# The first cross attention of a decoder: values and sums of a head in one product instead of two

## The chip, the cores and the metric

The kernel runs on one core of a Trainium2 chip. The metric is the device time of one launch in microseconds (us). Five runs of the kernel before took 1561.32 to 1566.45 us, with a median of 1562.86 us.

The engines are named as the profile names them: PE is the tensor engine (PEld its weight loads), DVE the vector engine, ACT the scalar engine, POOL the GpSimd engine, SP the engine that only issues transfers. SBUF is the working memory and PSUM the memory that the tensor engine writes; both have 128 partitions (rows).

## The reference, cut to what matters

The program is a two-layer decoder over 16 batches of 128 tokens and 256 features, in fp32. Layer 0 has a ternary self attention, a cross attention with rotary positions over the context and a mixture of experts; layer 1 has a latent attention, a second cross attention without projections and a gated product-key network. The change is in the cross attention of layer 0. There the input of a batch is read as 128 channels by 256 positions:

```python
q = jnp.einsum('oi,bit->bot', wq, x) + bq[None, :, None]
k = jnp.einsum('oi,bit->bot', wk, c) + bk[None, :, None]
v = jnp.einsum('oi,bit->bot', wv, c) + bv[None, :, None]
...
scores = jnp.einsum('bhqc,bhkc->bhqk', q, k) / math.sqrt(K_CHANNELS)
p_attn = jax.nn.softmax(scores, axis=-1)
out = jnp.einsum('bhqk,bhkc->bhqc', p_attn, v)
out = out.transpose(0, 1, 3, 2).reshape(b, CHANNELS, t_t)
out = jnp.einsum('oi,bit->bot', wo, out) + bo[None, :, None]
```

There are 16 heads of 8 channels, 256 queries and 256 keys. Query and key are turned by the rotary positions before the scores. The result is added to the input and normalised.

## The kernel before, in words

**Layout.** The 128 channels lie on the 128 partitions: four groups `g` of 32 rows, and in each group four heads of 8 rows. A score tile `ps_st` holds the transposed or plain scores of two groups and two heads. The transposed scores, with the row maximum already subtracted by a small product (`pick` and `nmT`), go through `Exp` on ACT (line 421) into `pT`, keys on partitions. The plain scores go only through a maximum on DVE (line 416), which fills `nm` for the next batch's subtraction.

**Sums.** For each unit `u` of a batch (a key half `kc`, a pair `i` of heads, one head `n` of the pair), `sums` (line 424) issues eight products into one PSUM tile `o` (`ps_o`), whose two halves are `o[:, 0, :]` for the weighted values and `o[:, 1, :]` for the sums of the weights. The first four (line 433), one for each group, have 32 columns of the value tile as stationary operand, in which only the 8 columns of this head are not zero; so the four heads of a group are gathered in the 32 rows of the group. The next four (line 437) have a tile of ones, `ones8`, in the place of the values, so that the sum of a head's weights stands on all 8 rows of that head. An fp32 product shows as two MATMUL records, so a unit shows as eight of `ps_o<-pT,v` and eight of `ps_o<-pT,ones`. A batch has eight units.

**Division.** `divided` (line 296) takes the logarithm of `o[:, 1, :]` on ACT (line 299), the exponential of its negative (line 300), and multiplies `o[:, 0, :]` by that on DVE (line 302) into `oT`, each over 256 elements a row. `cross_finish` (line 807) then multiplies by the output weights `xw[:, 5, :]`, and adds bias and input (line 811, `xn`); `normalised` (line 186) makes the new `x` with two statistics on DVE, a power on POOL (line 184) and a last DVE instruction (line 194).

**Values.** `values` (line 834) makes the projected values with PE and writes them with one DVE instruction (line 839) into one of three value tiles `v8`, whose other columns were zeroed by POOL at the start (line 75).

**The order of the work.** `by_beats` (line 242) writes the order out by hand. A batch of this attention takes eight beats, one for each unit. In a beat PE first makes scores for two batches (line 385): the transposed ones of one batch and the plain ones of a later one, by turns. Then come the sums of the unit whose scores were made two beats before, then the jobs of that beat. PE runs strictly in this order (`mm` and `turned`, lines 206 and 210). Of the jobs of line 853 each beat has one or two, and they return every eight beats. Here the beats of a batch period are lettered from the one with the division:

| beat | jobs | lines |
|---|---|---|
| A | last sums of a batch, then `divide`; `keys` of a later batch | 847, 831 |
| B | first sums of the next batch; `values` | 834 |
| C | `finish`, then the normalisation | 850 |
| D | `gate_turn`: turns the new `x` for the expert gate | 748 |
| E | `gate`: expert logits and the two best experts | 756 |
| F | `places`: where each token goes in the experts' lists | 782 |
| G | `maxima`: the maxima of a batch, split in three and turned | 844 |
| H | `queries` of a later batch | 824 |

DVE, ACT and POOL instructions are put in order by a planner at build time; on the chip each engine then works strictly in that order.

**What is shared.** The PSUM has eight banks. Score tiles rotate over three buffers of two banks each (line 235), two tiles a beat: a plain tile uses the buffer that the transposed tile of the beat before has left, so it waits for that tile's `Exp`; a transposed tile uses that of the plain tile two beats before and waits for its maximum. The jobs share one bank `ps_m`. The tile `o` has one buffer (line 227): the first sums of the next batch, in beat B, wait until the division has read `o` for the last time.

Of the kernel before, what the change touches and what calls it, by code (L numbers as in the profile page):

```python
# [18 lines left out]
P = 128  # L19
# [10 lines left out]
def kernel(ctx: ExitStack, tc: tile.TileContext, a: dict, out: bass.AP):  # L30
# [36 lines left out]
    def head_columns(pool, keys, heads, name, count=4):  # L67


        hd = 32 * 4 * (2 if keys == 1 else 1) // heads  # L70
        per = 32 // hd
        tiles = []
        for n in range(count):
            t = pool.tile([P, heads // per * keys, per * (32 + hd)], F32, name=f"{name}_{n}")
            nc.gpsimd.memset(t, 0.0)
            tiles.append(t)
        return tiles

    def max_columns(pool, name):

        tiles = []
        for n in range(2):
            t = pool.tile([P, 2, P], BF16, name=f"{name}_{n}")
            nc.gpsimd.memset(t, 0.0)
            tiles.append(t)
        return tiles
# [15 lines left out]
    causT = const.tile([P, P], BF16, name="causT")  # L102

    ones16 = const.tile([P, 2, 32], F32, name="ones16")
    ones8 = const.tile([P, 4, 32], F32, name="ones8")
    for t, per in ((ones16, 2), (ones8, 4)):
        nc.gpsimd.memset(t, 0.0)
        for i in range(per):
            nc.gpsimd.memset(t[:, i, i * 32 // per : (i + 1) * 32 // per], 1.0)

    v16 = head_columns(cpool, 1, 16, "v16")
    nmx = max_columns(cpool, "nmx")
# [10 lines left out]
    )  # L123
    onesb = const.tile([P, P], BF16, name="onesb")
    nc.gpsimd.memset(onesb, 1.0)
    v8 = head_columns(w0, 2, 16, "v8", 3)
    iota8 = const.tile([P, 8], F32, name="iota8")
    nc.gpsimd.iota(iota8, [[1, 8]], base=0, channel_multiplier=0, allow_small_or_imprecise_dtypes=True)

# [9 lines left out]
    nc.gpsimd.memset(zero, 0.0)  # L139


    xw = load(cpool, [P, 6, P], a["xw"], "xw", eng=nc.gpsimd)
    xb = load(cpool, [P, 5], a["xb"], "xb", eng=nc.gpsimd)
    bv2 = load(cpool, [P, D], a["bv2"].partition_broadcast(P), "bv2", eng=nc.gpsimd)
    rope = load(cpool, [P, 2, D], a["rope"], "rope", eng=nc.gpsimd)
# [60 lines left out]
    def mm(*args, **kw):  # L206

        tc.keep_in_program_order(nc.tensor.matmul(*args, **kw))  # L208
# [64 lines left out]
    def own_columns(t, hd):  # L273

        return t.rearrange("p g (i w) -> p g i w", w=32 + hd)[:, :, :, 0:hd]
# [20 lines left out]
    def divided(pl, o):  # L296
# [5 lines left out]
        nc.vector.tensor_tensor(oT.rearrange("p c q -> p (c q)"), o[:, 0, :], r, ALU.mult)  # L302
        return oT

    def rows_of(g):
        return slice(32 * g, 32 * g + 32)

# [71 lines left out]
    def cross_scores(pl, heads, kept):  # L379


        per = heads // 4
        onez = ones8 if per == 4 else ones16

        def beat(s, t):
            if t:
# [37 lines left out]
        def sums(b, u):  # L424
            z = kept[b]
            if u == 0:
                z["o"] = pl["o"].tile([P, 2, D], F32, name="ps_o")
            o, n = z["o"], u % 2
            kc, i = divmod(u // 2, per // 2)
            pTs = [z["pT"][u - n], z["pT"][u - n + 1]]  # L430
            first, last = u == 0, u == heads // 2 - 1
            for g in range(4):
                mm(
                    o[rows_of(g), 0, :], lhsT=z["v"][:, 4 * kc + g, 32 * (2 * i + n) : 32 * (2 * i + n) + 32],
                    rhs=pTs[g // 2][:, g % 2, n, :], start=first, stop=False,
                )
            for g in range(4):
                mm(
                    o[rows_of(g), 1, :], lhsT=onez[:, 2 * i + n, :], rhs=pTs[g // 2][:, g % 2, n, :],
                    start=False, stop=last,  # L440
                )

# [361 lines left out]
                in_offset=None,  # L804
            )

    def cross_finish(pl, b, oT):
        po = pl["m"].tile([P, D], F32, name="ps_m")
        mm(po, lhsT=xw[:, 5, :], rhs=oT.rearrange("p c q -> p (c q)"), start=True, stop=True)
        xn = pl["w"].tile([P, D], F32, name="xn")  # L810
        nc.vector.scalar_tensor_tensor(xn, po, xb[:, 4:5], x_t[b], ALU.add, ALU.add)
        normalised(x_t[b], xn)

    def rope_cross_plain(pl):
# [42 lines left out]
    def rope_cross_masked(st):  # L857
# [3 lines left out]
        for b in range(B):  # L861
# [19 lines left out]
            cross_finish(pl, b, oT)  # L881
            for part in (gate_turn, gate, places):
                part(pl, b)

# [533 lines left out]
def layouts(inputs):  # L1418
# [15 lines left out]
    masks += [((row % 32 < 12) & (row % 4 == j)) * 1.0 for j in range(4)]  # L1434
    wq, wk, wv, wo = (i[f"L0_xattn_w{n}"] for n in "qkvo")
    bq, bk, bo = (i[f"L0_xattn_b{n}"] for n in "qko")
    mask = i["mask_1x1x2048x2048_if1"][0, 0]
    return {
        "x": i["x"],
# [7 lines left out]
        "xw": np.stack([wq.T, wq[mate].T, wk.T, wk[mate].T, wv.T, wo.T], 1),  # L1447
# [45 lines left out]
```

## Time and profile before

| what | value |
|---|---|
| median of five runs | 1562.86 us |
| the profiled execution | 1564.26 us |
| its span, first to last instruction | 1562.1 us |
| PE busy | 1408.4 us (90%) |
| DVE busy | 807.9 us (52%) |
| ACT busy | 555.3 us (36%) |
| POOL busy | 265.6 us (17%) |
| first cross attention, scores to last placement | about 170 to 590 us |
| one batch period in it, beat A to beat A | 23.42 us |

The span is what lies between the first and the last instruction; 2.2 us of the profiled execution lie around it. The busy shares are means over the whole program, in which the attentions (to about 590 us, and from 960 to 1300 us), the experts (600 to 900 us) and the last network follow each other. A MATMUL's recorded end is modelled, and neighbouring products overlap, so the steps of PE are read from start to start.

### The profile page before, as it was taken

The numbers are of one execution on the slowest core, as the hardware profiler recorded it, in microseconds if no ns is written. First come the engines' busy times: TensorE is split into PE (matmuls) and PEld (weight loads), VectorE is DVE, ScalarE is ACT, GpSimd is POOL, SyncE is SP. The second block draws the span as 40 slices with busy tenths as digits, with TensorE's granted clock in tenths as the row PEclk, the third lists the DMA queues.
The fourth block names the chain that finished last, engine by engine and source line by source line (L and its number), as shares of the span: only waits on it lengthen the run. The fifth ranks groups of instructions, "written<-read, shape, count | busy, mean of one in ns | idle before, by whom it ended". The sixth has DMA issues, their size and how long they took to land. (4 is left out here: it accounts for less than half of the span.)

```text
span 1562.1 us, 30539 instructions
## 1 busy us (share of the span) xinstructions
PE 1408.4 (90%) x13003; PEld 880.4 (56%) x13003; DVE 807.9 (52%) x2210; ACT 555.3 (36%) x939; POOL 265.6 (17%) x370
## 2 busy tenths in 40 slices
PE   4999889999999977999999859899899998989997
PEld 3666545555555534777777636555555544446756
DVE  6788767677677630011111046776666655553322
ACT  1444334444444431111111124443355554772010
POOL 7001122332332210000000043321111200000000
PEclk9999989999999997999999959999999998999999
DMA  8200000000000005233320141100000000000000
GB/s 290 74 2 2 2 1 8 15 15 9 15 15 8 15 15 180 88 94 111 95 92 34 36 139 29 28 9 2 1 2 2 2 2 1 1 0 8 21 4 24
DMA packets 41689, 58.16 MB, mean 37 GB/s; under 512 B 4752, under 2 KB 31392, under 8 KB 41408
## 3 DMA queue, kind: packets, MB, share of 16 engines
q1 hardware_dynamic: 35984, 41.95, 8.2%
q0 software_dynamic: 4720, 13.29, 2.6%
q8 instruction: 106, 1.74, 0.5%
q10 hardware_dynamic: 832, 0.79, 0.2%
q14 instruction: 47, 0.39, 0.1%
HBM read 39.24 MB, written 16.78 MB: 36 GB/s over the span
## 5 line engine op out<-in xcount | busy, mean ns | idle before, releaser
L416 DVE TENSOR_REDUCE nm<-ps_st 128x4 f32<-128x1024 f32 x192 | 233.9, 1222 | 98.0 <-PE ps_st L208 97.5
L421 ACT ACTIVATE pT<-ps_st 128x1024 f32<-128x1024 f32 x192 | 196.5, 1023 | 246.5 <-PE ps_st L208 246.5
L184 POOL TENSOR_TENSOR rstd<-ve,nhalf 128x1 f32<-128x1 f32 x112 | 62.5, 558 | 713.3 <-DVE ve L183 697.2
L208 PE MATMUL ps_o<-pT,v 128*32 128x256 f32 (+1 forms) x2560 | 165.2, 347 | 1.1 <-DVE oT L302 0.8
L208 PE MATMUL ps_o<-pT,ones 128*32 128x256 f32 x2048 | 158.5, 380 | 0.0
L943 DVE TENSOR_TENSOR ye<-ps_e,b 128x256 f32<-128x256 f32 x40 | 17.0, 425 | 265.1 <-PE ps_e L940 265.1
L208 PE MATMUL ps_st<-rot,z 32*128 32x256 f32 x1024 | 147.5, 408 | 5.1 <-DVE nm L416 4.7
L928 PE MATMUL ps_h<-h,w 128*128 128x320 f32 x512 | 139.1, 432 | 0.0
L932 ACT ACTIVATE h<-ps_h,b 128x640 f32<-128x640 f32 x64 | 50.7, 793 | 228.7 <-PE ps_h L928 228.7
L208 PE MATMUL ps_st<-z,rot 32*128 32x512 f32 x512 | 131.9, 592 | 0.0
L928 PEld LDWEIGHTS ps_h<-h,w 128*128 128x128 f32 x512 | 97.3, 190 | 40.5
L208 PE MATMUL ps_st<-nmT,pick 32*128 32x256 bf16 x1024 | 103.7, 275 | 18.0 <-ACT nmT L293 15.7
L208 PEld LDWEIGHTS ps_o<-pT,v 128*32 128x32 f32 x2560 | 55.2, 109 | 104.4 <-issue 87.4
L208 PEld LDWEIGHTS ps_st<-rot,z 32*128 32x128 f32 x1024 | 89.5, 188 | 11.8 <-DVE nm L416 5.5
L352 DVE TENSOR_REDUCE nm<-ps_st 128x8 f32<-128x1024 f32 x64 | 78.1, 1220 | 34.5 <-PE ps_st L208 34.5
L1039 POOL DMA_INDIRECT y<-ys,place x32 | 31.1, 973 | 313.0 <-DVE absT L1031 305.3
L208 PEld LDWEIGHTS ps_o<-pT,ones 128*32 128x32 f32 x2048 | 65.7, 110 | 33.0
L208 PEld LDWEIGHTS <-pick 32*128 32x128 bf16 x1024 | 33.5, 91 | 83.0 <-issue 76.3
L928 PE MATMUL ps_h<-xeT,w 128*128 128x320 f32 x256 | 72.9, 443 | 2.3 <-DVE xeT L918 1.1
L208 PE MATMUL ps_st<-ctx,z 32*128 32x256 f32 x512 | 72.1, 398 | 0.5 <-DVE nm L416 0.4
L940 PE MATMUL ps_e<-w,h 128*128 128x256 f32 x320 | 70.4, 379 | 0.0
L208 PE MATMUL ps_f<-fxT,fgw 128*128 128x512 f32 x128 | 62.7, 613 | 6.7 <-ACT g L1215 6.7
(271 smaller groups left out, 2437.3 us busy)
## 6 DMA issues: line engine op xcount, KB each, us to landing
w<-in_W_dram SPq DMA_DIRECT2D x16, 512.0 KB, 4.1
w<-in_W_dram SPq DMA_DIRECT2D x8, 1024.0 KB, 5.3
xs<-zero SPq DMA_DIRECT2D x40, 128.0 KB, 4.7
xe<-xs SPq DMA_DIRECT2D x40, 128.0 KB, 3.7
ys<-ye SPq DMA_DIRECT2D x40, 128.0 KB, 2.0
x<-in_x_dram SPq DMA_DIRECT2D x16, 128.0 KB, 6.4
ctx<-in_ctx_dram POOLq DMA_DIRECT2D x16, 128.0 KB, 5.3
out_dram<-x SPq DMA_DIRECT2D x16, 128.0 KB, 1.7
```

The costliest lines, as they stand in the source:

```text
L184: in_order(nc.gpsimd.tensor_tensor(dst, ve, nhalf, ALU.pow))
L208: tc.keep_in_program_order(nc.tensor.matmul(*args, **kw))
L352: nc.vector.tensor_reduce(zs["nm"].rearrange("p c g n -> p g c n")[:, gs : gs + 2], ps, AX.X, ALU.max, negate=True)
L416: nc.vector.tensor_reduce(zs["nm"][:, qc, gs : gs + 2, js : js + 2], ps, AX.X, ALU.max, negate=True)
L421: nc.scalar.activation(pT, pt, AF.Exp)
L928: nc.tensor.matmul(ps[:, n, 0:H], lhsT=w[:, c, hc * P : (hc + 1) * P], rhs=src[:, c, n * H : (n + 1) * H], start=(c == 0), stop=(c == part ...
L932: nc.scalar.activation(dst[:, hc, :].rearrange("p (n t) -> p n t", n=2), ps[:, :, 0:H], AF.Gelu, bias=b12[:, layer, e, hc : hc + 1],)
L940: nc.tensor.matmul(ps, lhsT=h2[:, fc, c * P : (c + 1) * P], rhs=w3[:, fc, :], start=(fc == 0), stop=(fc == 3))
L943: nc.vector.tensor_add(ye[:, c, :], ps, b3[:, e, :])
L1039: in_order(nc.gpsimd.indirect_dma_start(out=y, out_offset=None, in_=ys[:, :], in_offset=bass.IndirectOffsetOnAxis(ap=place[:, b, n : n + 1 ...
```

## The change

In the first cross attention alone:

- The value tiles get another shape: for each group and head 32 columns of their own. In the columns of head `n` of a pair, 8 columns at `8 n` hold the values and 8 columns at `16 + 8 n` hold ones, put there once by POOL at the start; the rest is zero.
- `sums` issues four products a unit instead of eight. A product gathers the values of a pair's heads in rows 0 to 15 of a group, and their sums in rows 16 to 31. The first pair goes to `o[:, 0, :]`, the second to `o[:, 1, :]`. `o` keeps its size and its one buffer.
- `divided_pairs` moves the sums to the rows of the values: a `stream_shuffle` on DVE of all 512 elements a row, from PSUM into an SBUF tile `l`. Logarithm and exponential on ACT then work on `l`, and the DVE multiplication reads `o` and `l`, all three over 512 elements a row instead of 256.
- `values` writes with two DVE instructions of half the size instead of one.
- `finish` multiplies twice, once for each pair, with output weights whose rows are rearranged and, in rows 16 to 31 of each group, zero. `xw` grows from six to eight matrices (384 to 512 KB).
- `ones8` is gone. The second cross attention, the latent and the ternary attention keep their separate products with ones.

```diff
+    def value_and_one_columns(pool, name, count):
+        tiles = []
+        for n in range(count):
+            t = pool.tile([P, 8, 4, 32], F32, name=f"{name}_{n}")
+            nc.gpsimd.memset(t, 0.0)
+            for i in range(4):
+                nc.gpsimd.memset(t[:, :, i, 16 + 8 * (i % 2) : 24 + 8 * (i % 2)], 1.0)
+            tiles.append(t)
+        return tiles
...
-    v8 = head_columns(w0, 2, 16, "v8", 3)
+    v8 = value_and_one_columns(w0, "v8", 3)
...
-    xw = load(cpool, [P, 6, P], a["xw"], "xw", eng=nc.gpsimd)
+    xw = load(cpool, [P, 8, P], a["xw"], "xw", eng=nc.gpsimd)
...
+    def divided_pairs(pl, o):
+        l = pl["w"].tile([P, 2, D], F32, name="l")
+        nc.vector.stream_shuffle(l, o, [n % 16 + 16 for n in range(32)])
+        nc.scalar.activation(l, l, AF.Ln)
+        nc.scalar.activation(l, l, AF.Exp, scale=-1.0)
+        nc.vector.tensor_tensor(l, o, l, ALU.mult)
+        return l
...
+            if per == 4:
+                for g in range(4):
+                    mm(
+                        o[rows_of(g), i, :], lhsT=z["v"][:, 4 * kc + g, 2 * i + n, :], rhs=pTs[g // 2][:, g % 2, n, :],
+                        start=first, stop=last,
+                    )
+                return
...
-    def cross_finish(pl, b, oT):
+    def cross_finish(pl, b, *products):
         po = pl["m"].tile([P, D], F32, name="ps_m")
-        mm(po, lhsT=xw[:, 5, :], rhs=oT.rearrange("p c q -> p (c q)"), start=True, stop=True)
+        for n, (w, oT) in enumerate(products):
+            mm(po, lhsT=xw[:, w, :], rhs=oT, start=(n == 0), stop=(n == len(products) - 1))
...
-            nc.vector.tensor_tensor(
-                own_columns(v, 8), pv.rearrange("p c (g i d) -> p (c g) i d", g=4, i=4),
-                bv2.rearrange("p (g i d) -> p g i d", g=8, i=4), ALU.add,
-            )
+            for n in range(2):
+                nc.vector.tensor_tensor(
+                    v[:, :, n::2, 8 * n : 8 * n + 8],
+                    pv.rearrange("p c (g i n d) -> p (c g) i n d", g=4, i=2, n=2)[:, :, :, n, :],
+                    bv2.rearrange("p (g i n d) -> p g i n d", g=8, i=2, n=2)[:, :, :, n, :], ALU.add,
+                )
...
         def divide(b):
-            kept[b] = divided(pl, kept[b]["o"])
+            kept[b] = divided_pairs(pl, kept[b]["o"])
...
         def finish(b):
-            cross_finish(pl, b, kept.pop(b))
+            oT = kept.pop(b)
+            cross_finish(pl, b, (6, oT[:, 0, :]), (7, oT[:, 1, :]))
```

More of the change, by code (lines that the diff above doesn't have):

```diff
@@ L104 @@
     ones16 = const.tile([P, 2, 32], F32, name="ones16")
[L105 to L109, printed above, removed]
+    nc.gpsimd.memset(ones16, 0.0)
+    for i in range(2):
+        nc.gpsimd.memset(ones16[:, i, i * 16 : (i + 1) * 16], 1.0)
     v16 = head_columns(cpool, 1, 16, "v16")
@@ L382, in cross_scores @@
         per = heads // 4
-        onez = ones8 if per == 4 else ones16
         def beat(s, t):
@@ L438, in sums @@
                 mm(
-                    o[rows_of(g), 1, :], lhsT=onez[:, 2 * i + n, :], rhs=pTs[g // 2][:, g % 2, n, :],
+                    o[rows_of(g), 1, :], lhsT=ones16[:, 2 * i + n, :], rhs=pTs[g // 2][:, g % 2, n, :],
                     start=False, stop=last,
@@ L880, in rope_cross_masked @@
             oT = cross_heads(pl, 16, rot[0], [z[:, i, :] for i in range(4)], v, dict(masked, v=vn))
-            cross_finish(pl, b, oT)
+            cross_finish(pl, b, (5, oT.rearrange("p c q -> p (c q)")))
             for part in (gate_turn, gate, places):
@@ L1436, in layouts @@
     bq, bk, bo = (i[f"L0_xattn_b{n}"] for n in "qko")
+    pairs = []
+    for n in range(2):
+        pairs.append(np.where((row % 32 < 16)[:, None], wo.T[(row // 32 * 32 + 16 * n + row % 16)], np.float32(0.0)))
     mask = i["mask_1x1x2048x2048_if1"][0, 0]
@@ L1446, in layouts @@
         "w0": np.stack([i[f"L0_attn_w_{n}"].T for n in "qkvo"], 1),
-        "xw": np.stack([wq.T, wq[mate].T, wk.T, wk[mate].T, wv.T, wo.T], 1),
+        "xw": np.stack([wq.T, wq[mate].T, wk.T, wk[mate].T, wv.T, wo.T] + pairs, 1),
         "xb": np.stack([bq, bq[mate], bk, bk[mate], bo], 1),
```

## The prediction

> **What bounds the kernel now.** First the page's busy times, to see which engine can be the bound at all:
>
> ```profile
> PE 1408.4 (90%) x13003; PEld 880.4 (56%) x13003; DVE 807.9 (52%) x2210; ACT 555.3 (36%) x939; POOL 265.6 (17%) x370
> ```
>
> PE is the candidate. A mean over stages settles nothing, so next the busy time of each engine (PE, PEld, DVE, ACT, POOL, then clock and DMA) in one batch period of the changed stage:
>
> ```profile
> 303.52:326.94 23.42, 22.33 (x281) 12.33 (x280) 16.79 (x43) 10.06 (x14) 8.27 (x11) 1.00 0.04 13
> ```
>
> PE is busy for 22.33 of 23.42 us; DVE has 6.6 us to spare. Then the timeline of beat A, from its sums to those of beat B:
>
> ```profile
> 301.52 0.64 PE L208 MATMUL ps_o<-pT,v 128*32 128x256 f32 x8
> 301.70 1.02 ACT L421 ACTIVATE pT<-ps_st 128x1024 f32<-128x1024 f32 x1 [2.23 <-PE ps_st L208]
> 301.70 1.23 DVE L416 TENSOR_REDUCE nm<-ps_st 128x4 f32<-128x1024 f32 x1 [0.38 <-PE ps_st L208]
> 301.98 0.61 PE L208 MATMUL ps_o<-pT,ones 128*32 128x256 f32 x8
> 302.52 1.13 PE L208 MATMUL ps_m<-ctx,xw 128*128 128x256 f32 x4
> 302.66 0.38 ACT L299 ACTIVATE r<-ps_o 128x256 f32<-128x256 f32 x1
> 303.07 0.42 ACT L300 ACTIVATE r<-r 128x256 f32<-128x256 f32 x1
> 303.52 0.42 DVE L302 TENSOR_TENSOR oT<-ps_o,r 128x256 f32<-128x256 f32 x1 [0.60 <-ACT r L300]
> 303.58 0.28 PE L208 MATMUL ps_st<-nmT,pick 32*128 32x256 bf16 x2
> 304.76 0.64 PE L208 MATMUL ps_o<-pT,v 128*32 128x256 f32 x8
> ```
>
> Values take 0.46 us of PE (301.52 to 301.98), ones 0.54, keys 1.06, the scores 1.18. The division lets `ps_o` go at 303.94, 0.82 us before beat B's first sums want it: PE does not wait. Where it does, the list of PE's waits over 13 periods (line waited for, total, times, longest) tells:
>
> ```profile
> PE ps_st L208 <- ACT nmT L293: 6.0, 13, 0.5
> PE ps_m L211 <- DVE x L194: 4.7, 13, 0.4
> PE ps_m L208 <- DVE both L779: 3.5, 13, 0.3
> ```
>
> Three waits a period (beats H, D, F), each short, each at the end of a chain through DVE or ACT. If PE gets faster, these chains are late next.
>
> **The change part by part.** I write V for the start of a beat's value products: A 301.52, B 304.76, C 307.59, D 310.40, E 313.39, F 316.11, G 318.76, H 321.69, next A 324.94. Without ones, what follows V comes after 0.54 us instead of 0.46 + 0.54 = 1.00: 0.46 off PE in each beat, 8 x 0.46 = 3.68 us a period. `finish` goes from two MATMUL records to four of the same form; keys' four take 1.06 us against 0.63 for two (308.59 to 309.22), so it adds 0.43. PE alone would gain 3.25 us a period. Beat by beat less is left.
>
> *A to B, the division's chain.* DVE's maximum starts at V + 0.18 and takes 1.22; a following instruction starts 0.09 before its end (as the maximum at 311.69 after `x`), so at V + 1.31. No shuffle is in the trace. Of its size from PSUM I take the copy of line 918, 128x512, 0.69 us; ends are 0.42 (line 607, 128x512 in SBUF) and 1.22 (the maximum, 128x1024). I add 0.08 for loading its pattern, as MATCH_VALUE_LOAD before FIND_INDEX8 (316.55 to 316.62); the other end is 0. So the shuffle ends at V + 2.08. ACT's two run on 512 elements from SBUF: line 300's 0.42 plus 256 more elements at 0.83 ns (from 0.38 at 256 and 1.02 at 1024) makes 0.63 each; with 0.03 us between them as now, 2.11 to 2.74 and 2.77 to 3.40. The multiplication takes 0.68 (line 694, 128x512 from PSUM): 3.43 to 4.11. A product released by `oT` starts 0.05 later (558.78 + 0.43 to 559.26). B's V is A's V + 4.16; now it is + 3.24. PE would be there at 2.78, and now waits 1.38 us. This interval grows by 0.92.
>
> The Trainium skill, VectorE: DVE Perf Modes, section on the perf-mode tier table, has STREAM_SHUFFLE at 1x only, about 2400 ns for 2048 elements; with the page's 0.96 GHz that is an estimate of 0.80 us for 512, which would make the interval 0.11 longer and the whole forecast 1.6 us slower than the copy's row does.
>
> *B to C:* 0.54 + 0.65 (values) + 1.18 = 2.37 instead of 2.83: -0.46. The two DVE writes of `v`, 0.27 to 0.42 each (a 128x128 scalar product takes 0.27, line 670; the old instruction 0.42), hide in DVE's idle 0.83 us before C's maximum.
>
> *C to E:* `xn` started 1.74 after C's V; now 1.74 - 0.46 + 0.43 = 1.71. From there statistics, POOL's power and `x` run as before, and D's `gate_turn` waits for them: 5.80 becomes 5.77. PE's gains in two beats are lost to a longer wait for `x`.
>
> *E to G:* the expert logits are ready at E's V + 0.54 + 0.65 = 1.19, but DVE is in the maximum until 1.31, against 1.65 now. The chain of small DVE instructions to `both` keeps its length: 5.37 becomes 5.03.
>
> *G to H:* `nmT` is copied behind `Exp` on ACT, which ends at G's V + 1.20; now it starts at 1.32 (320.08). 2.93 becomes 2.81. *H to A:* queries, no wait: 3.25 becomes 2.79.
>
> Sum for a period: +0.92 - 0.46 - 0.03 - 0.34 - 0.12 - 0.46 = -0.49 us, 23.42 to 22.93. DVE is then busy for 16.79 + 0.77 + 0.26 + 0.16 = 18 us of it and ACT for 10.06 + 0.46: neither is the bound, their order is.
>
> From batch 0's division (beat A at 231.27) to batch 13's there are 13 periods: -6.4. Before them four beats already wait for `Exp` (the plain scores at 219.23 start 0.25 after the pick) and only G and H gain: -0.6. The fourteenth, whose second half has no plain scores (they end at 546), gives -0.8: as the others, and 0.33 more at G, where the copy of `nmT` started 0.46 late (552.96) and now comes right behind `Exp`. In the tail (556.75 on) no maximum holds the shuffle: A to B grows by 1.06, B, E and F give 0.95, the last sums 0.8; the last division has no cover, and 0.80 (shuffle) + 0.46 (ACT) + 0.26 (multiplication) + 0.43 (finish) = 1.95 are on the path: +1.26. Together -6.5 us. At the start POOL has twelve more small memsets (0.09 each, line 109), six fewer of ones and smaller `v` tiles (3.36 us for 128x1280 x3, so 0.7 less), and 128 KB more of `xw`; behind it wait only loads for later, since POOL's own first `rstd` waits 31.5 us for DVE: 0 to 0.5 us if that cover went. ACT, SP and the experts' loads are untouched. The profiled run was 1564.26 (span 1562.1 and 2.2 around it), 1.4 above the median; on the median the forecast is 1562.86 - 6.5 = 1556.4 us.
>
> **The clock.** A wait of PE can cost more than itself. Lines of 3.4 us (PE busy first, clock after the engines):
>
> ```profile
> 189.58:192.99 3.41, 1.50 (x10) 0.88 (x10) 3.38 (x11) 0.00 (x0) 0.00 (x0) 1.00 0.00 0
> 193.00:196.40 3.40, 2.47 (x12) 1.45 (x12) 3.33 (x8) 0.04 (x1) 0.00 (x0) 0.50 0.00 0
> 1019.02:1022.43 3.41, 2.25 (x14) 1.40 (x14) 2.61 (x7) 0.75 (x3) 1.97 (x3) 1.00 0.02 4
> 1022.44:1025.84 3.40, 3.40 (x42) 2.39 (x44) 1.60 (x7) 0.87 (x2) 1.07 (x2) 0.50 0.24 71
> 1111.18:1114.59 3.41, 1.87 (x28) 1.20 (x22) 1.89 (x5) 1.02 (x1) 0.55 (x1) 1.00 0.00 0
> 1114.60:1118.00 3.40, 2.28 (x38) 1.27 (x34) 2.55 (x7) 1.53 (x2) 0.00 (x0) 1.00 0.02 5
> ```
>
> After 1.50 us of busy PE the clock fell to half; after 2.25 it fell once; after 1.87 it held. In beat B PE idles from V + 2.85, where the recorded ends of the scores lie, to 4.16: 1.31 us, which leaves 2.10 busy in such a line. That is between the rows. I take it as holding.
>
> The Trainium skill, TensorE: Matmul & The Clock Gate, section HAM oscillation, gives the rule "no PE-idle gaps >~3.4µs". By it a gap of 1.31 costs nothing and the sum stays 1556.4; the rows above say that the clock falls after much shorter gaps, and by them up to 31 us are at stake (below).
>
> **The rivals.**
>
> *The waits cost the clock (slower).* If 2.10 us in a line is too little, each gap that lies whole in one line, (3.41 - 1.31) / 3.41 = 0.62 of 15, so 9, halves the clock. At 1022.44 it was for one line, from 193 for four. Half a line lost is 1.7 us; two lines each make 9 x 3.4 = 31: 1587 us; one each 1572. It decides if the division's chain passes about V + 4.3, since 1.87 us of busy PE held once. For it: the fall after 2.25. Against: that 1.87 held.
>
> *The multiplication stands behind B's maximum.* On the chip that maximum is ready at V + 2.96, before the multiplication at 3.43. If the planner puts it first, B waits until V + 4.83, 0.67 more a period, or -0.49 becomes +0.18: about 1566 with the tail, and PE then idles 1.98, so near the 1.50 row. Against it: at 311.37 `x` stands ahead of a maximum that was ready 0.8 us earlier, so the planner takes PE for slower than it is.
>
> *The shuffle stands before A's maximum.* It would run from V + 0.75, the chain would end at 3.5, and the period shrink by 1.1: 13 x 1.1 + 0.8 less 0.7 in start and tail is 15 to 17 us: 1546. Against it: the maximum is ready 0.5 us earlier.
>
> *PE is all that counts.* 16 x 3.25 = 52 us: 1511. The list of waits speaks against it: the chains behind D, F and H are already late.
>
> *The waits eat it all.* A shuffle of 1.22 us instead of 0.69 adds 0.53 a period, 7 us in all: 1563.
>
> **How the numbers follow.** About 0.2%, 3 us, is what can be told from no change: 1559.7 to 1566. The forecast, between 1552 and 1561 with its own unknowns (shuffle 0.42 to 0.8, `rot` of the keys behind the multiplication 0.22 a period), gets 0.45, of which 0.05 lie within 0.2%. Shuffle first, 0.07; PE alone, 0.01: faster. Waits eat it, 0.10: same. Clock, 0.27, of which 0.03 with so few falls that it looks the same; late multiplication, 0.10: slower but for 0.01. So faster 0.48, same 0.19, slower 0.33. The range goes from 1546 to 1586; below lie some 0.05, above some 0.12.
>
> **What will show it.** `ps_o<-pT,ones` has 1024 records fewer; a period is about 22.9 us; in beat B PE waits some 1.4 us for DVE `l`; the waits for `x` and `both` grow by about 0.5 and that for `nmT` by 0.3; a shuffle takes about 0.7 us; PEclk stays 1.00 in the stage. I am wrong if the clock falls there, if DVE's order in beats A and B differs from the one used here, or if ACT or DVE take other times on 512 elements.

## The result, and the profile after

The change makes next to no difference: 1563.24 us (median of 36 runs, 1557.35 to 1576.21) against 1562.62 us (62 runs, 1557.22 to 1567.36). The ratio is 1.0011, with a 95% interval of 1.0001 to 1.0020, so the changed kernel is slower by 0.2% at most and not faster. The forecast was 1556.4 us.

The profiled execution of the changed kernel took 1571.28 us, with a span of 1569.6 us and a mean granted clock of 0.955, so it is one of the slower ones. Each run comes with its mean clock: runs of the changed kernel at 0.957 to 0.960 took 1557.35 to 1567.31 us, those at 0.954 or 0.955 took 1565.91 to 1571.28, those at 0.946 to 0.951 took 1568.37 to 1576.21. Within the first of these groups the time does not follow the clock: the runs at 0.959 or 0.960 have a median of 1563.1 us, those at 0.957 or 0.958 one of 1562.0. The runs of the kernel before, beside the experiments below, all lay between 0.958 and 0.963. Two things are to be looked at: the beats, and the clock.

**The beats.** First the page's busy times. PE has 35.4 us less than before, and 992 fewer products (1024 of `ones` gone, 32 more in `finish` twice):

```profile
PE 1373.0 (87%) x12011; PEld 860.1 (55%) x12011; DVE 820.6 (52%) x2258; ACT 560.1 (36%) x939; POOL 265.8 (17%) x377
```

One batch period, from one multiplication of the division to the next (columns as before: PE, PEld, DVE, ACT, POOL, clock, DMA share, GB/s):

```profile
303.79:326.87 23.08, 19.46 (x218) 10.80 (x218) 17.62 (x46) 10.37 (x15) 6.27 (x9) 1.00 0.04 13
```

PE is busy for 2.87 us less, but the period is only 0.34 us shorter. The list of PE's waits over thirteen periods shows where the rest stands:

```profile
PE ps_o L219 <- DVE l L323: 18.0, 13, 1.4
PE ps_m L222 <- DVE x L205: 10.3, 13, 0.8
PE ps_m L219 <- DVE both L806: 10.1, 13, 0.8
PE ps_st L219 <- ACT nmT L304: 8.7, 13, 0.7
```

The first wait is new: 1.38 us a period for the division. The other three went from 0.36, 0.27 and 0.46 us to 0.79, 0.78 and 0.67. The timeline from beat A's sums to beat B's shows the new wait's chain:

```profile
300.37 0.64 PE L219 MATMUL ps_o<-pT,v 128*32 128x256 f32 x8
...
300.55 1.23 DVE L436 TENSOR_REDUCE nm<-ps_st 128x4 f32<-128x1024 f32 x1 [0.38 <-PE ps_st L219]
...
301.70 0.73 DVE L320 STREAM_SHUFFLE l<-ps_o 128x512 f32<-128x512 f32 x1
...
302.46 0.63 ACT L321 ACTIVATE l<-l 128x512 f32<-128x512 f32 x1 [0.89 <-DVE l L320]
...
303.12 0.63 ACT L322 ACTIVATE l<-l 128x512 f32<-128x512 f32 x1
303.66 1.00 ACT L441 ACTIVATE pT<-ps_st 128x1024 f32<-128x1024 f32 x1
303.79 0.69 DVE L323 TENSOR_TENSOR l<-ps_o,l 128x512 f32<-128x512 f32 x1 [0.60 <-ACT l L322]
304.39 1.22 DVE L436 TENSOR_REDUCE nm<-ps_st 128x4 f32<-128x1024 f32 x1
...
304.62 0.42 PE L219 MATMUL ps_o<-pT,v 128*32 128x256 f32 x4 [1.37 <-DVE l L323]
```

The shuffle waits for the maximum, ACT's two for the shuffle, the multiplication for these, and beat B's products for the multiplication, 4.25 us after beat A's. Behind it beat B's maximum stands, as the prediction had it.

**The clock.** The page's row of the granted clock (40 slices of 39.2 us) has a 7 in the slice from 549 to 589 us, where the kernel before had a 9:

```profile
PEclk9999989999999977999999958999999998999999
```

In the last two batches, in the two profiles taken of the changed kernel, the falls last 3.41, 6.83 and 20.48 us, which is one, two and six times 3.41; so the stage is cut into lines of that length that begin and end with the falls. In such lines (PE busy first, clock after the engines), around the divisions of the last two batches and with one line of a full period at the top:

```profile
510.75:514.16 3.41, 1.99 (x26) 1.18 (x26) 2.48 (x5) 1.74 (x3) 2.46 (x3) 1.00 0.00 0
...
531.23:534.64 3.41, 1.56 (x20) 0.80 (x16) 2.05 (x4) 2.49 (x4) 0.00 (x0) 1.00 0.11 38
534.64:538.05 3.41, 2.99 (x22) 1.99 (x26) 1.90 (x4) 0.46 (x1) 0.00 (x0) 0.50 0.02 5
538.05:541.47 3.42, 3.42 (x20) 1.50 (x15) 1.22 (x1) 1.02 (x1) 0.00 (x0) 0.50 0.00 0
...
555.12:558.53 3.41, 2.46 (x20) 0.57 (x16) 0.72 (x2) 2.39 (x5) 0.27 (x1) 1.00 0.12 41
558.53:561.95 3.42, 2.56 (x16) 0.92 (x16) 0.69 (x1) 0.90 (x1) 0.00 (x0) 0.50 0.00 0
561.95:565.36 3.41, 3.41 (x14) 1.38 (x12) 0.00 (x0) 1.02 (x1) 0.00 (x0) 0.50 0.00 0
```

In the full periods the clock stays whole, in lines with as little as 1.99 us of busy PE. In the last two batches, where the work for later batches runs out, it falls twice to half, each time for two lines, right behind a line in which PE waits for the division (1.84 us for the first, which lies mostly in the line; 1.8 for the second, half in it). What is missing at the first of these two, the fourteenth division, is `keys`: beat A still has plain scores, but no `keys` of a later batch, and so PE comes sooner to beat B's products and waits 1.84 us instead of 1.38:

```profile
530.78 0.64 PE L219 MATMUL ps_o<-pT,v 128*32 128x256 f32 x8
...
535.06 1.08 PE L219 MATMUL ps_o<-pT,v 128*32 128x256 f32 x8 [1.84 <-DVE l L323]
```

In the kernel before, the lines at and just ahead of the same beats have 2.59 to 3.41 us and the clock holds:

```profile
534.24:537.65 3.41, 3.32 (x50) 1.68 (x46) 1.98 (x3) 2.17 (x4) 0.97 (x1) 1.00 0.11 40
...
551.39:554.80 3.41, 2.59 (x30) 1.08 (x32) 0.00 (x0) 1.44 (x3) 1.44 (x2) 1.00 0.11 38
554.80:558.21 3.41, 3.41 (x46) 1.50 (x40) 0.00 (x0) 2.23 (x3) 0.55 (x1) 1.00 0.14 46
```

**An account of the stage.** The first `xn` (the residual sum after `finish`) comes between 231.4 and 239.5 us in the profiles of this study, and in two profiles of the same changed kernel at 239.5 and 235.3. So ends can't be compared to a few microseconds, and lengths are read instead, in three parts: from the first `xn` to beat H ahead of the fourteenth division (called the full periods), from there to the last values' products (the last two batches; the sums of the last three units follow each other directly, and the first of them is meant), and from these to the last `xn` (the end).

| profile | a period | full periods | last two batches | end | sum |
|---|---|---|---|---|---|
| before | 23.42 | 293.36 | 40.17 | 5.31 | 338.84 |
| after | 23.09 | 288.96 | 46.17 | 7.31 | 342.45 |

The full periods win 4.4 us. The last two batches and the end lose 8.0. What comes behind the last `xn` takes 984.2 us before and 987.7 after, but 982.2 in the second profile of the same changed kernel, so that difference is not the change's. Of the 46.17 us, 5.7 come from the two falls: four intervals between beats are stretched to 4.41, 3.72, 3.26 and 4.08 us, and the same intervals take 2.39, 2.81, 1.75 and 2.81 in profiles whose clock is whole there (scores twice, filled end, VectorE's copy, below). Put in, these leave 40.46. This is an estimate from single intervals; the experiments give it another way.

### The profile page after: what moved, and what is told of

Read it like the earlier page. It is cut to its first block, busy times and chain, and to the rows that moved or that the text cites. A ratio compares the mean times of both kernels' runs of the same rounds, so it can differ in the third digit from the quotient of the medians.

```text
span 1569.6 us, 28624 instructions
## 1 busy us (share of the span) xinstructions
PE 1373.0 (87%) x12011; PEld 860.1 (55%) x12011; DVE 820.6 (52%) x2258; ACT 560.1 (36%) x939; POOL 265.8 (17%) x377
## 5 line engine op out<-in xcount | busy, mean ns | idle before, releaser
L219 PE MATMUL ps_o<-pT,ones 128*32 128x256 f32 x1024 | 79.1, 381 | 0.0
L971 PEld LDWEIGHTS ps_e<-w,h 128*128 128x128 f32 x320 | 60.8, 190 | 9.1
```

What stands on the lines that cost most here:

```text
L971: nc.tensor.matmul(ps, lhsT=h2[:, fc, c * P : (c + 1) * P], rhs=w3[:, fc, :], start=(fc == 0), stop=(fc == 3))
```

## Theory and rivals

The theory after reading: the chain of the division takes most of what the products win, about as forecast, and what is left is lost again in the last two batches, because there the clock falls. Rivals: the products win nothing at all, because the waits for `x`, `both` and `nmT` would take any gain; the division does not set beat B; or the clock falls for other reasons, and filling PE's waits changes nothing. The first four runs test sizes, the others the clock.

### The products alone, and the division alone

The first kernel is the changed one with a division in the shapes of before:

```diff
+    def divided_small(pl, o):
+        r = pl["w"].tile([P, D], F32, name="r")
+        nc.scalar.activation(r, o[:, 1, :], AF.Exp, scale=1e-4)
+        nc.scalar.activation(r, r, AF.Exp, scale=-10.0)
+        oT = pl["w"].tile([P, 2, P], F32, name="oT")
+        nc.vector.tensor_tensor(oT.rearrange("p c q -> p (c q)"), o[:, 0, :], r, ALU.mult)
+        return oT
...
-            kept[b] = divided_pairs(pl, kept[b]["o"])
+            kept[b] = divided_small(pl, kept[b]["o"])
...
-            cross_finish(pl, b, (6, oT[:, 0, :]), (7, oT[:, 1, :]))
+            cross_finish(pl, b, (5, oT.rearrange("p c q -> p (c q)")))
```

> The changed kernel with the division of before (no shuffle, two ACT operations and one multiplication over 128x256, one product in the finish). The computation is changed: both ACT operations are exponentials that make a small constant, and half of each pair of heads is left out of the output, so the first cross attention adds almost nothing; the instructions have the shapes of before. Theory (the long division takes the gain, the values' products keep it): ps_o is free about 2.4 us after V, the wait of 1.37 us a period in front of beat B goes, A to B falls from 4.25 to about 2.9 us, the period from 23.08 to 21.6 (one finish product fewer too), 14 periods give about -20 us: 1540 to 1546. Rival (the gain of the products is taken by other waits of the period whatever the division does): the waits on x, both and nmT grow by as much, period 22.9 to 23.4, time 1558 to 1566.

Measured: 1538.14 us (1531.34 to 1541.59, 4 runs), ratio 0.9857 (0.9836 to 0.9878). The period is 21.20 us, A to B 2.81, and PE no longer waits for the division in the full periods. The waits for `x`, `both` and `nmT` are what they are in the changed kernel (0.8, 0.8 and 0.7 us). So the first rival falls: the gain of the products is there, and the time lies below the forecast. The period is 1.89 us shorter than the change's; 1.47 of that lie in A to B, the rest in C to D (2.38 against 2.81), where `finish` has one product fewer.

The second kernel is the one before with the long division alone:

```diff
-            kept[b] = divided(pl, kept[b]["o"])
+            o = kept[b]["o"]
+            l = pl["w"].tile([P, 2, D], F32, name="l", bufs=1)
+            nc.vector.stream_shuffle(l, o[:, 1:2, :].to_broadcast([P, 2, D]), list(range(32)))
+            nc.scalar.activation(l, l, AF.Ln)
+            nc.scalar.activation(l, l, AF.Exp, scale=-1.0)
+            nc.vector.tensor_tensor(l, o, l, ALU.mult)
+            kept[b] = l
...
-            cross_finish(pl, b, kept.pop(b))
+            cross_finish(pl, b, kept.pop(b)[:, 0, :].rearrange("p (c q) -> p c q", c=2))
```

> The kernel before, with values and ones in separate products, and the long division alone: the row of sums shuffled onto itself twice (128x512), Ln, Exp and multiplication over 128x512; the finish reads one half. Theory (ps_o is held until 4.25 us after V): A to B goes from 3.24 to about 4.3 us, period 23.42 to about 24.4, 14 periods give +14 us: 1575 to 1580, more if the longer wait also lets the clock fall (up to 1590). Rival (the wait is set by something else than the division, the chain is covered by PE work): 1561 to 1566.

Measured: 1587.66 us (1585.21 to 1594.11, 4 runs), ratio 1.0162 (1.0141 to 1.0183). The period is 24.43 us, A to B 4.27, and PE's waits over thirteen periods have a line that the kernel before has not, 0.95 us a period:

```profile
PE ps_o L208 <- DVE l L853: 12.4, 13, 1.0
```

Thirteen periods at 1.01 are 13 us. The median rose by 25.5, and the runs' mean clock was 0.954 to 0.962. In its profile the clock fell from 574.2 to 601.5 us, in the last two batches, which took 53.24 us instead of 40.17. So the wait lengthens A to B as the chain says, and in this profile it costs more than itself at the end. But two of the four runs had mean clocks of 0.960 and 0.962, as the kernel before has, and still took 1585.21 and 1586.60 us: falls of the clock are not all of what lies above the 13 us, and the rest is not explained.

### Taking the wait away

If beat B waits for `ps_o` alone, a copy of `ps_o` in SBUF frees it early. In these kernels and in the one with the division alone, the tile `l`, and a tile of the same name elsewhere in the kernel, also have one buffer only. One kernel copies on VectorE behind the shuffle:

```diff
         nc.vector.stream_shuffle(l, o, [n % 16 + 16 for n in range(32)])
+        oc = pl["w"].tile([P, 2, D], F32, name="oc", bufs=1)
+        nc.vector.tensor_copy(oc, o)
         nc.scalar.activation(l, l, AF.Ln)
         nc.scalar.activation(l, l, AF.Exp, scale=-1.0)
-        nc.vector.tensor_tensor(l, o, l, ALU.mult)
+        nc.vector.tensor_tensor(l, oc, l, ALU.mult)
```

> The changed kernel, with ps_o copied by VectorE into SBUF right after the shuffle (about 0.7 us) and the multiplication reading the copy; so ps_o is free about 2.8 us after V and not 4.0. Theory (beat B's products wait for the division): the wait in front of them goes from 1.37 to 0 to 0.3 us, A to B 2.9 to 3.1 us, period 21.7 to 22.0, 14 periods give -15 to -19 us: 1544 to 1549. Rival 1 (VectorE's chains of x and of the gate set the period): the waits on x, both and nmT take it, period 22.6 to 23.1, time 1556 to 1564. Rival 2 (the copy delays the key products and the maximum of beat B behind it on VectorE by 0.7 us each period): period 23.4 to 23.8, time 1568 to 1574.

Measured: 1551.76 us (1540.02 to 1556.99, 9 runs), ratio 0.9938 (0.9914 to 0.9962); the period is 21.91 us. The timeline of a period around beat B:

```profile
293.93 0.72 DVE L320 STREAM_SHUFFLE l<-ps_o 128x512 f32<-128x512 f32 x1
...
294.56 0.67 DVE L322 COPY oc<-ps_o 128x512 f32<-128x512 f32 x1
...
295.41 0.64 PE L219 MATMUL ps_o<-pT,v 128*32 128x256 f32 x8
...
296.01 1.02 DVE L325 TENSOR_TENSOR l<-oc,l 128x512 f32<-128x512 f32 x1
```

Beat B's products now start 0.6 us ahead of the multiplication, without a wait. The first rival to this run falls: the other waits do not grow. The second has a small part: B to C takes 2.65 us instead of 2.39, since the plain scores of beat C start 0.06 us after the `Exp` of beat B has ended, and that stands behind the division's two ACT operations (296.95 after 296.89). The profile's stage is 17.0 us shorter than before (321.86 against 338.84). But the median won only 10.4 us, less than the 13 to 18 expected, and the mean clocks of the runs were 0.948 to 0.960: the fastest run, 1540.02 us, had 0.960, and the five at 0.948 or 0.949 took 1550.34 to 1556.32.

The other copies on ScalarE ahead of the shuffle; its multiplication reads `oc` too:

```diff
         l = pl["w"].tile([P, 2, D], F32, name="l", bufs=1)
+        oc = pl["w"].tile([P, 2, D], F32, name="oc", bufs=1)
+        nc.scalar.copy(oc, o)
         nc.vector.stream_shuffle(l, o, [n % 16 + 16 for n in range(32)])
```

> The changed kernel, with ps_o copied into SBUF by ScalarE ahead of the shuffle (about 0.65 us beside VectorE's maximum) and the multiplication reading the copy. Theory (beat B waits for ps_o alone): ps_o is free when the shuffle ends, about 2.1 us after V, the wait is gone and nothing is added to VectorE; period 21.5 to 21.9, against 21.92 with VectorE's copy; with clock falls as in that run 1545 to 1553. Rival (ScalarE's copy delays the exponentials behind it, so that scores or sums wait): period 22.3 or more, 1558 or more.

Measured: 1557.96 us (1546.99 to 1564.09, 12 runs), ratio 0.9969 (0.9946 to 0.9992). The wait for the division is gone here too, but the period is 22.26 us, not 21.5 to 21.9. In the waits over the same stretch another line takes part of its place, about 0.4 us a period, as this run's rival said:

```profile
PE ps_st L219 <- ACT pT L443: 7.3, 16, 0.7
```

The plain scores of beat C wait for the exponential of beat B, which stands behind the division's two ACT operations. With VectorE's copy this line has 0.8 us in all, for the list leaves out waits below 0.15 us. Here the shuffle also came only when ScalarE's copy had ended.

### Where the clock falls

One kernel repeats products in beat B of every period, where PE waits:

```diff
+            if s and per == 4 and s[1] == 4:
+                for n in range(2):
+                    for g in range(2):
+                        mm(
+                            ps[:, g, n, :], lhsT=zs["qz"][rows_of(gs + g), js + n, qc * P : (qc + 1) * P],
+                            rhs=zs["k"][rows_of(gs + g), :], start=True, stop=True,
+                        )
```

> The changed kernel, and in beat B of each period the four plain score products are issued once more (same result), so that PE streams for about 0.5 us more in the stretch in which it waits 1.37 us for the division. Theory (the missing microseconds are falls of the granted clock in the stage, brought by the long waits): the period stays 23.0 to 23.1, no line of the stage falls to half clock, the mean clock stays at .957 or above, the slow end of the runs (1566 to 1576) is gone, median 1557 to 1561. Rival (the clock falls come from elsewhere, or more work only costs): median 1563 to 1570 and the same spread of clocks, .946 to .960.

Measured: 1567.00 us (1558.45 to 1574.31, 12 runs), ratio 1.0034 (1.0015 to 1.0052), clocks 0.948 to 0.961. The period is 23.07 us and PE's wait for the division half as long (0.63 us), but the clock is no better. Its profile says why:

```profile
529.70:533.12 3.42, 2.32 (x28) 1.57 (x24) 2.06 (x4) 2.50 (x4) 0.00 (x0) 1.00 0.08 26
...
543.36:546.77 3.41, 2.54 (x26) 0.80 (x25) 2.78 (x20) 1.42 (x3) 0.00 (x0) 1.00 0.00 0
546.77:550.18 3.41, 2.95 (x20) 1.08 (x18) 0.04 (x1) 1.40 (x2) 1.35 (x2) 0.50 0.11 38
```

At the fourteenth division, where the plain scores could still be repeated, the line has 2.32 us of PE and the clock holds. It falls some 13 us later, in beats that have no plain scores and so nothing that this kernel repeats, and stays at half for ten lines, to 580.9. The last two batches took 51.35 us, 10.9 more than the 40.46. I had filled the full periods, which did not need it.

A second profile of the unchanged change was to show whether the falls keep their place:

> The changed kernel once more, for a second profile, since the first is of a run at a mean clock of .955 and most runs have .957 to .960. Theory (falls in the last two batches): with a mean clock of .959 or .960 no fall, or one short one, between 500 and 575 us, the twelve periods 23.07 to 23.1 as in the first profile, the last two batches 40 to 42 us; with .955 or less the falls are there again. Rival (the clock is lost in other stages): the last two batches take 46 us at any mean clock.

Measured: 1564.54 us at a mean clock of 0.955. The period is 23.09 us again, the last two batches 49.21. Again it falls behind the fourteenth division, and again among the beats without plain scores:

```profile
527.74:531.15 3.41, 1.41 (x20) 0.90 (x22) 2.05 (x5) 2.29 (x4) 0.00 (x0) 1.00 0.00 0
531.15:534.57 3.42, 3.42 (x28) 2.21 (x20) 1.23 (x3) 0.00 (x0) 0.00 (x0) 0.50 0.02 5
541.39:544.81 3.42, 2.54 (x26) 1.32 (x28) 2.93 (x19) 1.87 (x4) 0.00 (x0) 1.00 0.00 0
544.81:548.22 3.41, 3.30 (x18) 0.81 (x15) 0.93 (x7) 1.10 (x2) 1.02 (x1) 0.50 0.11 38
```

That answers for a clock of 0.955; a run at 0.959 or 0.960 has not been seen in a profile. The run that decides fills the last two batches alone. In the pairs, the first number is the batch of the transposed scores, counted from 0, the second its unit: 2 is beat B, 4 is D, 6 is F, 7 is G.

```diff
-            for n in range(2):
+            again = per == 4 and t in ((14, 2), (14, 6), (14, 7), (15, 2), (15, 4), (15, 6))
+            for n in (0, 1, 0, 1) if again else (0, 1):
                 if t:
```

> The changed kernel, with the score products of six beats of the last two batches (the ones at the divisions and at the gates, where there are no scores of a next batch) issued a second time with the same result, and nothing else: the twelve full periods are untouched. Theory (what the twelve periods win, 4 us, goes in the last two batches, where lines with long waits let the clock fall to half; 5.4 us in the profile of the change, 10.9 in the one with scores twice): no fall between 500 us and the end of the stage, the last two periods take 40 to 43 us instead of 46, median 1557 to 1560, highest run below 1566. Rival (the falls do not come from waits in these beats, or the extra products cost what they save): median 1562 to 1566, highest above 1570.

Measured: 1560.03 us (1557.86 to 1563.20, 12 runs), ratio 0.9987 (0.9975 to 0.9999). All twelve runs have mean clocks of 0.959 to 0.962, and the slow end of the change's runs is gone. The full periods are the same to 0.01 us (288.96). The last two batches take 42.29 us. The clock holds through both divisions:

```profile
529.15:532.56 3.41, 2.65 (x38) 1.51 (x34) 1.89 (x3) 2.14 (x3) 0.00 (x0) 1.00 0.02 5
532.56:535.98 3.42, 3.42 (x44) 2.09 (x40) 2.28 (x5) 1.02 (x1) 0.00 (x0) 1.00 0.00 0
...
553.04:556.46 3.42, 2.66 (x27) 1.06 (x26) 0.64 (x1) 1.78 (x2) 0.00 (x0) 1.00 0.00 0
556.46:559.87 3.41, 3.41 (x28) 1.45 (x26) 1.66 (x5) 0.54 (x2) 0.57 (x1) 1.00 0.00 0
```

So 56 more product records that compute nothing new make the changed kernel faster, and its twelve runs lie within 5.3 us, where 36 of the change lie within 18.9. The control is the same edit in the kernel before:

> The kernel before with the same second issue of the scores in the six beats of the last two batches: the control for the extra products. Theory (they help only where the clock would fall, and before's clock holds to the end of the stage): they cost about what they cost without a fall, 1 to 3 us: 1563 to 1566. Rival (the extra products help by something else than the clock): 1556 to 1560, faster than before, as in the changed kernel.

Measured: 1566.31 us (1565.30 to 1570.67, 7 runs), ratio 1.0035 (1.0018 to 1.0053): 4.1 us slower, more than I had put, and the last two batches are 4.58 us longer (44.75). There the extra products only cost. In the changed kernel they cost too, and win it back: that speaks for the clock and against any other use of them.

### Both cures together

ScalarE's copy, with the extra products in the six beats:

> ScalarE's copy of ps_o and the second issue of the scores in the six beats of the last two batches, together. Theory: period 21.5 to 21.9 and no fall in the last two batches: 1538 to 1545, spread under 10 us. Rival (the falls are not to be had this way): as with the copy alone, 1545 to 1557.

Measured: 1549.48 us (1543.96 to 1553.44, 6 runs), ratio 0.9920 (0.9898 to 0.9943). The period is 22.26 us, as with ScalarE's copy alone, so the forecast for it was too low; the clocks are 0.957 to 0.962 instead of 0.947 to 0.961, and the median is 8.5 us better than without the extra products. The profiled run of ScalarE's copy alone took 1557.57 us, close to its median, so here the falls of a run near the median can be seen: the clock is at half from 531.1 to 596.0 us, 19 lines on end, of which the lines below show the start, and the last two batches take 49.39 us.

```profile
527.71:531.13 3.42, 2.31 (x24) 0.97 (x21) 1.90 (x14) 1.93 (x2) 0.71 (x1) 1.00 0.01 2
531.13:534.54 3.41, 2.98 (x16) 0.89 (x15) 0.00 (x0) 0.93 (x3) 1.28 (x2) 0.50 0.11 38
```

With the extra products the clock holds until 558.0 us, 3.4 us ahead of the last `xn`, and the last two batches take 40.64 us: 8.75 us less, about as much as the medians differ by.

VectorE's copy, with the same six:

> VectorE's copy of ps_o and the second issue of the scores in the six beats of the last two batches, together. Theory (the copy frees beat B, the extra products hold the clock to the end of the stage): period 21.9, no fall of the clock before the stage's end, the last two batches about 2 to 4 us longer than undisturbed ones; mean clock .957 or above in all runs, median 1541 to 1547 and a spread under 10 us. Rival (with less work a period the clock falls whatever stands in these beats): as with the copy alone, 1548 to 1553, clocks down to .948.

Measured: 1542.64 us (1540.38 to 1545.88, 4 runs), ratio 0.9881 (0.9854 to 0.9908), clocks 0.959 to 0.961, a period of 21.9 us.

And VectorE's copy with three of them:

```diff
-            again = per == 4 and t in ((14, 2), (14, 6), (14, 7), (15, 2), (15, 4), (15, 6))
+            again = per == 4 and t in ((14, 6), (15, 4), (15, 6))
```

> The same with extra products in three of the six beats only, the ones where PE waits for the gate and for x in the last two batches; the two beats behind a division, where the copy has taken the wait away, and beat G have none. Theory (a fall needs a wait in a beat without a next batch's scores): three beats are enough, 1540 to 1546. Rival (the whole of the last batches has too little PE work): the clock falls in part of the runs, 1545 to 1553, spread above 10 us.

Measured: 1541.54 us (1540.51 to 1542.70, 4 runs), ratio 0.9867 (0.9845 to 0.9890), clocks 0.959 to 0.961. Its last two batches take 38.58 us, the shortest of the complete kernels, and its clock, whole since 204.4 us, next falls at 552.5, 2.6 us ahead of the last `xn`, behind a line in which the stage's work runs out. This is the fastest version that computes the whole reference, 21.6 us below the kernel before beside it (1563.15).

```profile
545.72:549.14 3.42, 3.22 (x36) 1.14 (x38) 1.40 (x10) 2.05 (x2) 0.93 (x1) 1.00 0.02 5
549.14:552.55 3.41, 1.00 (x12) 0.33 (x12) 1.57 (x4) 1.26 (x2) 1.06 (x2) 1.00 0.13 47
552.55:555.96 3.41, 2.07 (x4) 1.17 (x4) 1.21 (x3) 0.00 (x0) 0.00 (x0) 0.50 0.09 30
```

The page gives its busy times:

```profile
PE 1366.8 (89%) x12035; PEld 856.3 (56%) x12035; DVE 830.4 (54%) x2274; ACT 559.9 (36%) x939; POOL 267.9 (17%) x377
```

PE has hardly less to do than in the changed kernel (1373.0 us busy). What differs is what it waits for, and at which clock it runs.

| kernel | median us | ratio | period | last two batches in the profile | mean clocks of the runs |
|---|---|---|---|---|---|
| after | 1563.24 | 1.0011 | 23.09 | 46.17 and 49.21 | 0.946 to 0.960 |
| scores twice in beat B | 1567.00 | 1.0034 | 23.07 | 51.35 | 0.948 to 0.961 |
| last batches filled | 1560.03 | 0.9987 | 23.09 | 42.29 | 0.959 to 0.962 |
| copy on VectorE | 1551.76 | 0.9938 | 21.91 | 38.84 | 0.948 to 0.960 |
| copy on VectorE, three beats filled | 1541.54 | 0.9867 | 21.91 | 38.58 | 0.959 to 0.961 |

## Why the prediction failed

**The chain from A to B: right in each step but the last.** From A's V the shuffle began at 1.33 (predicted 1.31), Ln at 2.09 (2.11), Exp at 2.75 (2.77), the multiplication at 3.42 (3.43), for 0.69 (0.68). The shuffle took 0.725 us and its pattern 0.014, where 0.69 and 0.08 had been taken. The step that was short: "A product released by `oT` starts 0.05 later" became 0.14 (304.48 to 304.62), and over all periods A to B has a median of 4.28 instead of 4.16.

**The other beats.** B to C 2.39 (2.37), C to E 5.79 (5.77), E to G 5.10 (5.03), G to H 2.70 (2.81), H to A 2.81 (2.79). What follows V comes after 0.57 us and not 0.54. Together the period lost 0.33 us and not 0.49: the mechanism held, the difference of a large gain and a large loss was a third smaller. Over the full periods that makes 4.4 us where the same working, without A to C of the first batch (+0.46) and H to A of the last period (-0.46), gives 13 x 0.49 + 0.46 - 0.46 = 6.4: 2.0 us too many.

**The ends.** From the first score of the stage to the first `xn` it takes 68.77 us in the first profile of the change and 68.48 before: +0.3, where the prediction's terms for this stretch (-0.6, and +0.43 from the first division to its `xn`) make -0.2. The last two batches, estimated without falls (40.46), and the end of the filled kernel (6.36, against 5.31 before) make +1.3, where the fourteenth batch (-0.8), the tail (+1.26) and the last H to A (-0.46) make 0. The term that was most in error here is "as the others", said of the fourteenth batch: its A to B has no `keys` to cover the chain and grows from 2.51 to 4.28 us, by 1.77 and not 0.92, and the H to A ahead of it gains nothing (2.33 us in both kernels). With these the sum is 0.3 - 4.4 + 1.3 = -2.8 us instead of -6.5, some 1559.8 from the median of before: at the bound of what can be told from no change.

**The steps that failed.** The forecast said -6.5 us, and +0.6 was measured. About half of the 7.1 us between them, 3.7, are terms that were mis-sized, as just listed: 2.0 in the full periods, the rest at the ends. The other half, 3.4, I put to the clock, a term that the prediction put at nothing. The words were "between the rows. I take it as holding", said of beat B in the full periods. There it was right: lines with 1.99 us, less than the 2.10 I had worked out, held in both profiles of the change. But the prediction weighed only this place. In the last two batches, which it priced at beats alone, the clock fell in both profiles and cost there 5.7 and, by the same measure, 8.7 us. Both profiles are of runs at 0.955. For the median run the price is an estimate: the median of the filled kernel is 3.2 us lower although its extra products cost about 1.8 us in the last two batches (42.29 against 40.46), which makes about 5 us. That with the -2.8 us would give 2 us more than before, and 0.6 were measured. No run of the changed kernel at 0.957 or above was profiled, and among these the time does not follow the clock, so it is not shown where the median run loses these microseconds; shown is that they come back when the last two batches are filled.

**Rows by busy PE were the wrong measure.** I read a bound from single lines: 1.50 fell, 1.87 held. The runs show lines with 1.99 that hold and lines with 2.46 and 2.54 that fall, and another line with 2.54 held (548.29 to 551.70 us in the first profile of the change). The Trainium skill, TensorE: Matmul & The Clock Gate, section HAM oscillation, which the prediction cited, would have no gap below about 3.4 us matter. The longest wait at the falls in the last two batches of the profile after is 1.84 us, so here the measurement decides against it. The same page's section on a second failure mode, psum-queue depth-cycling, says that frequent short idles between groups of products can make the clock swing too; that agrees with these lines, but gives no bound either.

**The rivals.** "The waits cost the clock" was right that the clock would fall behind such waits, but had the wrong beats and the wrong count: nine falls in fifteen periods were expected, none came in the full ones and two in the last batches, so its 1572 to 1587 us is reached only by the slowest runs, and only at its lower end. "The waits eat it all" names the measured time, but for another reason: the shuffle is 0.725 us, not 1.22. The estimate of 0.80 us that the prediction worked out from the Trainium skill (VectorE: DVE Perf Modes, the perf-mode tier table) is 0.075 above the measured row. The order on DVE was as assumed, so neither rival of order came. "PE is all that counts" is refuted by the chain, but the products with a short division win 24 us. That is 1.89 us a period more than the change, of which the chain has 1.47.

## What to carry to other kernels

A wait in which an engine sits ahead of a buffer is not priced by its length alone where PE's clock follows its work: look for the place with the least PE work beside the new wait, which here is the end of the loop and not its steady part. When a reformulation makes products cheaper and their consumer's chain longer, look first whether the buffer can be let go sooner; a copy of 0.67 us took away a wait of 1.38 us a period and shortened the period by 1.2. And a difference of two nearly equal numbers (here +0.92 and -1.41 a period) needs each to a few hundredths of a microsecond before its sign is worth a forecast.

## What was not expected of the hardware

- The clock's falls do not follow the busy time of a 3.41-us line alone: in the two profiles of the changed kernel the clock held behind lines of 1.99 us and behind one of 2.54, and fell behind lines of 1.41, 1.56, 2.46 and 2.54. Once at half it came back after one, two, six or ten lines, in the profiles of the change and of the scores twice, and after 19 in that of ScalarE's copy. What quantity decides stays open; that extra products in these beats hold it is shown, which property of them does so is not.
- The multiplication took 0.69 us with one operand in PSUM, and 0.97 us (median, 0.69 to 1.02) with both operands in SBUF behind VectorE's own copy; behind ScalarE's copy, with the same operands, it took 0.69. In the profiles with VectorE's copy, every one above 0.71 us ended 0.09 to 0.10 us after the end of a POOL instruction (line 858 or 859, which makes `z`) that had run beside it. So POOL's work beside it is the suspect; no run takes that work away.
- The first score of the stage came at 170.7 us in one profile of the changed kernel and at 166.6 in another. In these two profiles the start lies 4 us apart, more than the change is worth, which is why the stage's lengths were compared.
